# Layer a: a pair's own products moved up behind its key-value sums, ahead of the products with the state

## The chip, the cores and the metric

The kernel runs on one core of one Trainium2 chip. The metric is the time of one execution on the device, in microseconds (us). The engines are named as in the profile: PE multiplies matrices (PEld is its loading of weights), DVE, ACT and POOL are the vector, scalar and general engines, SP issues the DMAs.

## The reference

Four sub-layers with residual sums run over `x` of shape (4, 2048, 512). The change touches the first, a causal linear attention with 16 heads of 64:

```python
q = relu(x @ Wq) + EPS;  k = relu(x @ Wk) + EPS;  v = x @ Wv        # x: after layer norm
context = cumsum(einsum('bhnd,bhne->bhnde', k, v), axis=2)          # sums of keys times values
D_inv = 1.0 / einsum('bhnd,bhnd->bhn', cumsum(k, axis=2), q)
attn = einsum('bhnd,bhnde,bhn->bhne', q, context, D_inv)
x = x + attn @ Wo + bo
```

Behind it come a quantised feed-forward product, a gated linear attention with decays (layer b) and the feed-forward product again.

## The kernel before

A flag read at run time chooses between two forms of the layers; the profiled one is `layer_a_mild` and then `layer_b_mild`. Layer a ends about 2450 us into the span, layer b takes the rest.

`layer_a_mild` works on 16 blocks (`n`, 0 to 15) of 512 rows, and in each block on eight pairs of heads (`hp`, 0 to 7): 128 pairs. A block's 512 rows are four chunks of 128. The sum over earlier positions is split. What a chunk owes to earlier chunks goes through a running state per pair: `before[i]` is the state ahead of chunk `i`, and its product with the queries, four of 128x128 by 128 columns, is L968 ("the state's products" below). What a chunk owes to its own rows goes through masked scores: `scores` (L888) multiplies keys and queries, DVE multiplies the mask in (`sm`, L894, one tile for each of the two heads), and L974 multiplies the values with them ("the own products"): eight, each on 64 columns of the array, two heads side by side. Both are summed in one bank of PSUM, `pn` (one buffer, tag `n`), which ACT copies to `oT` (L983). `update` (L904) makes the sums of keys times values of each chunk, eight products on 64 columns of the array as well, which ACT copies to `u` (L909) and POOL adds up into `within` (L914, six additions), from which the state's products read.

Each f32 product stands as two PE instructions in the trace, so four of the state's products are x8 and eight of the own products x16.

`attend` returns a list of six steps for a pair: keys, scores, update, weigh, outputs, and an empty one. `spread` runs them in this order and puts one sixth of a list `fill` behind each step. `fill` holds the products that belong to no pair's chain: keys and queries of the next pair (`pk`, `pq`, four products each), values (`pv`, four), the projection of the block before (`po`, eight, for `hp` 0 to 3) or its feed-forward product (`pf`, for `hp` 4 to 7). The first `len(fill)/6` items stand behind keys, and so on. PE follows this order. On DVE, ACT, POOL and SP the order is set when the program is built, by a planner that takes what it expects to be ready first. In the trace there are steps of a later pair ahead of some of an earlier one.

For `hp` 3 and 7, `weigh` makes the divisors of four pairs: products with `same` (L926, bank `pd`), a logarithm and an exponential on ACT (L931, L933), two corrections on DVE (L935, L936), a store to DRAM (`rec`, L938) and loads that spread it over the partitions (`wide`, L959, one buffer, two pairs at a time). The four divisions `oT * wide` (L950) are put in the next pair's `fill` at places 6, 7, 13 and 15; the second one also issues the load for the last two. The projection of the block before reads the divided tiles: after `hp` 7 the four divisions lie in pair 0 of the next block, and so do the projection's first products.

Other lines that are named below: L804 takes a feature's product out of PSUM, L710 copies a tile into planes for the transposing DMA of L712, L717 joins the transposed planes (for `kr`, which `update` reads), L838 adds a projection to `x`, L124 and L125 take row statistics, L131 normalises, L664 to L670 quantise a row for the feed-forward product, L683 takes that product out, L733 loads the next block's `x`, L998 stores a finished block. In layer b, L1360 and L1373 are its update (`pub`) and outputs (`pyT`), which stand one right behind the other.

Of the kernel before, what the change touches and what calls it, by code (L numbers as in the profile page):

```python
# [10 lines left out]
F32 = mybir.dt.float32  # L11
# [8 lines left out]
P = 128  # L20
# [26 lines left out]
def hybrid_block_kernel(ctx: ExitStack, tc: tile.TileContext, t: dict, out: bass.AP):  # L47
# [4 lines left out]
    nc = tc.nc  # L52
# [16 lines left out]
    def banks(psum, **bufs):  # L69
        def bank(shape, dtype, name, tag):  # L70
            return psum.tile(shape, dtype, name=name, tag=tag, bufs=bufs[tag])

        return bank
# [97 lines left out]
    NTA = TA // P  # L171
# [464 lines left out]
    def run(steps):  # L636
        for f in steps:
            f()
# [83 lines left out]
    def layer_a_mild():  # L722
        with ExitStack() as es:
# [3 lines left out]
            bank = banks(psum, mm=3, s=2, n=1, u=1, t=1)  # L727
# [121 lines left out]
            def attend(B, hp):  # L849

                A = Block()
                chunks = [slice(i * P, (i + 1) * P) for i in range(NTA)]
                heads = [slice(h * DA, (h + 1) * DA) for h in range(2)]
                inner = within[hp % 2]
                vh = [slice((2 * hp + h) * DA % D, (2 * hp + h) * DA % D + DA) for h in range(2)]

                def v():
                    return B.v[hp // (NP // 2)]
# [97 lines left out]
                def load(rec, m):  # L956
# [2 lines left out]
                        nc.sync.dma_start(wide[r, :, :], rec[m : m + 2, h, :].partition_broadcast(DA))  # L959
                    return wide  # L960

                def outputs():


                    q = B.qk["q", hp]
                    pn = bank([P, NTA, P], F32, name="pn", tag="n")
                    for i in range(NTA):
                        nc.tensor.matmul(  # L968
                            pn[:, i, :], A.before[i], q[:, chunks[i]],
                            start=(i == 0), stop=False, skip_group_check=True,  # L970
                        )
                    for i in range(NTA):
                        for h, r in enumerate(heads):
                            nc.tensor.matmul(  # L974
                                pn[r, i, :], v()[:, i, vh[h]], A.sm[h][:, i, :],
                                start=False, stop=True, skip_group_check=True,
                            )
                    for r in heads:
                        nc.gpsimd.tensor_tensor(
                            A.before[0][r, r], A.before[NTA - 1][r, r], A.u[r, NTA - 1, :], ALU.add  # L980
                        )
                    B.oT[hp] = pool.tile([P, TA], F32, name="oT", bufs=12)
                    nc.scalar.copy(B.oT[hp], pn.rearrange("p i t -> p (i t)"))  # L983

                return [keys, scores, update, weigh, outputs, lambda: None]

            def block(n, x):
                B = Block()
                B.n, B.x, B.xn, B.qk, B.v, B.oT, B.mul, B.qc, B.kt = n, x, {}, {}, {}, {}, {}, {}, {}
                return B  # L990
# [15 lines left out]
            B, prev = block(0, x), None  # L1006
# [5 lines left out]
            for n in range(len(at)):  # L1012
# [6 lines left out]
                for hp in range(NP):  # L1019
# [20 lines left out]
                    for place, f in zip((6, 7, 13, 15), weights):  # L1040
                        fill.insert(place, f)
                    weights.clear()
                    spread(attend(B, hp), fill)
                    if n == 0:

# [10 lines left out]
                B = after if more else None  # L1056
# [640 lines left out]
```

## Time and profile before

| what | us |
|---|---|
| median of 3 runs (3968.38 to 3970.84) | 3969.62 |
| the profiled execution | 3970.43 |
| its span, first to last instruction | 3968.6 |
| PE busy in the span | 3886.1 |
| DVE busy | 2418.3 |
| POOL busy | 1504.4 |
| ACT busy | 879.2 |

The 1.8 us between the profiled execution and its span lie outside the first and last instruction. A matmul's row has a start and a modelled length; matmuls are pipelined, so what one costs is read from the start of one run of products to the start of the next.

### The profile page before, as it was taken

To read this page: it belongs to the slowest core of one execution; us is meant where nothing else is said; L and a number is where in the kernel's file an instruction comes from. 1 tells how busy PE (TensorE), PEld (TensorE's weight loads), DVE (VectorE), ACT (ScalarE), POOL (GpSimd) and SP (SyncE) were. 2 spreads that over 40 slices of the span, in tenths; PEclk is the share of its full clock that TensorE was granted. 3 is DMA by queue.
4 is the path that set the end of the run, shared out by engine and by line. 5 is a ranking of instruction groups with operands and counts; after the bars stand their busy time and mean duration, and the time that the engine had idled before them with its cause. 6 is when DMAs were issued, how large, how long until landed. Compare 5 with 4: busy or idle time off the path is not lost.

```text
span 3968.6 us, 53472 instructions
## 1 busy us (share of the span) xinstructions
PE 3886.1 (98%) x20765; PEld 2128.6 (54%) x20765; DVE 2418.3 (61%) x4552; ACT 879.2 (22%) x1550; POOL 1504.4 (38%) x2523
## 2 busy tenths in 40 slices
PE   7999999999999999999999996999999999999997
PEld 4555554555545555555555553666666666666664
DVE  4455555555555555554554554677777777777776
ACT  1221221221221221221222211222222222222221
POOL 3223323323233233233233223355555545555553
PEclk9999999999999999999999997999999999999999
DMA  4122222222212212212212214122212222222211
GB/s 139 30 41 54 67 41 54 67 40 54 67 39 55 67 39 55 67 39 55 67 39 55 57 29 144 23 54 54 55 50 51 52 53 54 55 50 51 53 37 32
DMA packets 430967, 216.97 MB, mean 55 GB/s; under 512 B 362736, under 2 KB 375920, under 8 KB 430704
## 3 DMA queue, kind: packets, MB, share of 16 engines
q1 hardware_dynamic: 429584, 211.89, 21.9%
q8 instruction: 165, 2.70, 0.3%
q10 hardware_dynamic: 1120, 1.57, 0.1%
q14 instruction: 98, 0.80, 0.1%
HBM read 91.49 MB, written 34.08 MB: 32 GB/s over the span
## 4 chain that ended last, share of the span: by engine, by line
PE 95%; DMA 2%; DVE 2%; POOL 1%; issue 0%; ACT 0%; SPq 0%; ACTq 0%; DVEq 0%; POOLq 0%
PE pr L1230 12%; PE pk L648 11%; PE pq L648 11%; PE pv L648 11%; PE po L648 11%; PE pvb L648 6%; PE py L1394 5%; PE pss L888 3%; PE ps L1326 3%; PE pn L974 3%; PE pg L648 3%; PE pl L1263 3%; PE pf L681 3%; PE pn L968 3%; PE pu L904 2%; PE pyT L1373 1%
## 5 line engine op out<-in xcount | busy, mean ns | idle before, releaser
L648 PE MATMUL pq<-xnTa,a_Wq 128*128 128x512 f32 x1024 | 492.2, 608 | 0.0
L648 PE MATMUL pk<-xnTa,a_Wk 128*128 128x512 f32 x1024 | 491.0, 604 | 0.0
L648 PE MATMUL pv<-a_Wv,xnTa 128*128 128x512 f32 x1024 | 476.6, 604 | 2.9 <-ACT xnTa L141 2.9
L648 PE MATMUL po<-a_Wo_sb,oT 128*128 128x512 f32 x1024 | 467.4, 601 | 7.2 <-DVE oT L950 7.1
L126 POOL TENSOR_SCALAR rs<-mv 128x1 f32<-128x1 f32 x320 | 82.3, 257 | 1019.4 <-DVE mv L125 1016.3
L914 POOL TENSOR_TENSOR within<-state,u 64x64 f32<-64x64 f32 x256 | 158.1, 618 | 523.4 <-ACT u L909 513.8
L648 PEld LDWEIGHTS po<-a_Wo_sb,oT 128*128 128x128 f32 x1024 | 189.3, 190 | 236.0 <-issue 220.0
L648 PEld LDWEIGHTS pv<-a_Wv,xnTa 128*128 128x128 f32 x1024 | 188.8, 191 | 234.4 <-issue 224.2
L648 PEld LDWEIGHTS pq<-xnTa,a_Wq 128*128 128x128 f32 x1024 | 181.4, 189 | 193.1 <-issue 182.8
L648 PEld LDWEIGHTS pk<-xnTa,a_Wk 128*128 128x128 f32 x1024 | 184.5, 189 | 180.9 <-issue 158.8
L909 ACT COPY u<-pu 128x256 f32<-128x256 f32 x128 | 47.7, 373 | 1026.9 <-PE pu L904 1026.9
L1230 PE MATMUL pr<-xnTb,m_kT_sb 128*128 128x256 f32 x1024 | 237.9, 385 | 0.0
L894 DVE TENSOR_TENSOR sm<-pss,causal 128x512 f32<-128x512 f32 x256 | 164.2, 683 | 119.8 <-PE pss L888 119.8
L1230 PE MATMUL pr<-xnTb,m_qT_sb 128*128 128x256 f32 x1024 | 237.2, 385 | 0.0
L717 ACT COPY kr<-turned 128x1024 uint16<-128x1024 uint16 x120 | 139.3, 1161 | 426.3 <-DMA turned<-planes 426.3
L648 PE MATMUL pvb<-b_vT_sb,xnTb 128*128 128x512 f32 x512 | 233.7, 599 | 0.0
L1394 PE MATMUL py<-b_oT_sb,yT 128*128 128x512 f32 x512 | 231.1, 594 | 0.0
L1339 DVE TENSOR_TENSOR ab<-ps,m_causal 128x512 f32<-128x512 f32 x256 | 164.1, 682 | 95.4 <-PE ps L1326 95.4
L1230 PEld LDWEIGHTS pr<-xnTb,m_qT_sb 128*128 128x128 f32 x1024 | 193.7, 192 | 32.6 <-ACT q L1294 0.2
L683 DVE SCALAR_TENSOR_TENSOR f_y<-pf,f_sc,rscale 128x512 f32<-128x512 f32 x126 | 94.5, 750 | 191.2 <-PE pf L681 191.0
L1230 PEld LDWEIGHTS pr<-xnTb,m_kT_sb 128*128 128x128 f32 x1024 | 189.4, 190 | 35.6 <-issue 12.3
L127 POOL TENSOR_TENSOR rs<-rs,neg_half 128x1 f32<-128x1 f32 x320 | 194.0, 607 | 26.3
(171 smaller groups left out, 6302.8 us busy)
## 6 DMA issues: line engine op xcount, KB each, us to landing
wide<-rec SPq DMA_DIRECT2D x124, 256.0 KB, 3.6
mmid<-xa SPq DMA_DIRECT2D x16, 1024.0 KB, 4.3
out<-xb SPq DMA_DIRECT2D x31, 512.0 KB, 2.8
xa<-in_x SPq DMA_DIRECT2D x15, 1024.0 KB, 6.6
xb<-mmid SPq DMA_DIRECT2D x30, 512.0 KB, 3.8
turned<-planes SPq DMA_TRANSPOSE x304, 3.1
m_cos<-in_cos SPq DMA_DIRECT2D x30, 128.0 KB, 2.5
m_sin<-in_sin SPq DMA_DIRECT2D x30, 128.0 KB, 2.3
```

The source lines that it names most:

```text
L127: nc.gpsimd.tensor_tensor(rs, rs, neg_half[:, :n], ALU.pow)
L648: nc.tensor.matmul(held[0], lhs(), rhs(), start=(n == 0), stop=(n == len(pairs) - 1))
L681: nc.tensor.matmul(pf, qT[:, c, :], rq[:, c, :], start=(c == 0), stop=(c == KC - 1))
L717: nc.scalar.copy(dst.bitcast(U16).rearrange("p n (t two) -> p n t two", two=2), turned.rearrange("p (two n) t -> p n t two", two=2),)
L888: nc.tensor.matmul(ps[h][:, i, :], k[r, chunks[i]], q[r, chunks[i]], start=True, stop=True)
L894: nc.vector.tensor_tensor(s, ps[h], causal.unsqueeze(1).to_broadcast([P, NTA, P]), ALU.mult)
L914: nc.gpsimd.tensor_tensor(A.before[i + 1][r, r], A.before[i][r, r], u[r, i, :], ALU.add)
L968: nc.tensor.matmul(pn[:, i, :], A.before[i], q[:, chunks[i]], start=(i == 0), stop=False, skip_group_check=True,)
L974: nc.tensor.matmul(pn[r, i, :], v()[:, i, vh[h]], A.sm[h][:, i, :], start=False, stop=True, skip_group_check=True,)
L1230: nc.tensor.matmul(pr[:, half, :], wp[name][:, c, lo : lo + P], B.xnT[:, c, :], start=(c == 0), stop=(c == KC - 1),)
L1339: nc.vector.tensor_tensor(C.a[:, half, :, :].rearrange("p h (j s) -> p h j s", s=QB), ps[half].rearrange("p j h s -> p h j s"), small["cau ...
L1394: nc.tensor.matmul(py, B.yT[i][:, c, :], wo[:, c, :], start=(c == 0), stop=(c == KC - 1))
```

## The change

The own products get a step of their own, `own`, which now opens the bank `pn` (`start` on its first products) and runs right behind `update`, with no fill between them. `outputs` keeps the state's products, which now close the bank, the last two additions to the state and the copy to `oT`. The list of steps changes too: the empty step moves up to third place, `update` with `own` is fourth, `weigh` fifth and `outputs` sixth. So update, weigh and outputs each stand one sixth of the fill later than before, and the own products one sixth earlier. No instruction is added or taken away.

```diff
+                def own():
+                    A.pn = bank([P, NTA, P], F32, name="pn", tag="n")
+                    for i in range(NTA):
+                        for h, r in enumerate(heads):
+                            nc.tensor.matmul(
+                                A.pn[r, i, :], v()[:, i, vh[h]], A.sm[h][:, i, :],
+                                start=(i == 0), stop=False, skip_group_check=True,
+                            )
+
                 def outputs():
-                    q = B.qk["q", hp]
-                    pn = bank([P, NTA, P], F32, name="pn", tag="n")
+                    q, pn = B.qk["q", hp], A.pn
                     for i in range(NTA):
                         nc.tensor.matmul(
                             pn[:, i, :], A.before[i], q[:, chunks[i]],
-                            start=(i == 0), stop=False, skip_group_check=True,
+                            start=False, stop=True, skip_group_check=True,
                         )
-                    for i in range(NTA):
-                        for h, r in enumerate(heads):
-                            nc.tensor.matmul(
-                                pn[r, i, :], v()[:, i, vh[h]], A.sm[h][:, i, :],
-                                start=False, stop=True, skip_group_check=True,
-                            )
...
-                return [keys, scores, update, weigh, outputs, lambda: None]
+                return [keys, scores, lambda: None, lambda: run([update, own]), weigh, outputs]
```

## The prediction

> **What bounds the kernel now.** I read the page's first part, the chain, and then layer a alone, by the busy time of a stretch and PE's waits.
>
> ```profile
> PE 3886.1 (98%) x20765; PEld 2128.6 (54%) x20765; DVE 2418.3 (61%) x4552; ACT 879.2 (22%) x1550; POOL 1504.4 (38%) x2523
> PE 95%; DMA 2%; DVE 2%; POOL 1%; issue 0%; ACT 0%; SPq 0%; ACTq 0%; DVEq 0%; POOLq 0%
> ```
>
> ```profile
> 166.00:2400.00 2234.00, 2230.99 (x11015) 1130.17 (x11018) 1211.89 (x2317) 484.09 (x652) 671.83 (x1428) 1.00 0.22 52
> ```
>
> ```profile
> PE po L648 <- DVE oT L950: 7.1, 4, 5.7
> PE pn L968 <- POOL within L914: 3.9, 7, 1.2
> ```
>
> In the stretch from 166 to 2400 us PE is busy 2231 of 2234 us, at a granted clock of 1.00; the next, DVE, 1212. PE's waits in all of layer a are a few us. So layer a lasts as long as PE's own sequence, and what the change does to that sequence is its effect, as long as no new wait arises. The sequence is read from the timeline of PE, here for pair 5 of a block (starts in the first column):
>
> ```profile
> 1638.93 1.88 PE L648 MATMUL pk<-xnTa,a_Wk 128*128 128x512 f32 x4
> 1640.74 1.16 PE L888 MATMUL pss<-qT,kT 64*128 64x128 f32 x16
> 1641.83 1.98 PE L648 MATMUL pk<-xnTa,a_Wk 128*128 128x512 f32 x4
> 1643.74 0.69 PE L904 MATMUL pu<-va,kr 128*64 128x64 f32 x16
> 1644.36 3.70 PE L648 MATMUL pq<-xnTa,a_Wq 128*128 128x512 f32 x8
> 1647.90 0.38 PE L968 MATMUL pn<-qT,state 128*128 128x128 f32 x2
> 1648.12 0.83 PE L968 MATMUL pn<-qT,within 128*128 128x128 f32 x6
> 1648.88 1.09 PE L974 MATMUL pn<-sm,va 128*64 128x128 f32 x16
> 1649.91 3.70 PE L648 MATMUL pv<-a_Wv,xnTa 128*128 128x512 f32 x8
> ```
>
> A 512-column instruction takes 0.43 us, a 128-column one 0.11. What is over these is the price of going between the whole array (128\*128) and parts of it (64\*128, 128\*64). Going in: 1638.93 to 1640.74 is 1.81 = 4 x 0.43 + 0.09. Coming out costs twice: own products 1.03, of which seven steps take 0.82 (1.09 less the last one's 0.27), the last pair streams 0.10, and 0.10 is idle; then the first whole-array run is 0.10 longer than its products (1641.83 to 1643.74 is 1.91 against 1.81).
>
> **What PE's sequence loses.** Before, update and own products are two excursions per pair; after, one. Per pair:
> - The idle behind update: its last product starts at 1643.74 + 0.69 - 0.23 (one product's mean) = 1644.20, the next run 0.16 later.
> - The 0.10 that the first run behind update is longer (q x8: 3.54 against 8 x 0.43 = 3.44).
> - The 0.09 of going in ahead of the own products: the state's x8 take 0.98 against 8 x 0.11 = 0.89. After the change they stand between whole-array products and cost 0.89.
> - The own products' first step is longer (0.16) than the later ones (0.10), since the second weights only load while it streams.
>
> In their place stands a join of update and own products, which layer a's trace doesn't have. Layer b has its like, also between products of 64 and of 128 columns on equal parts of the array:
>
> ```profile
> 2976.28 0.32 PE L1360 MATMUL pub<-vb,kt 128*32 128x64 f32 x8
> 2976.41 0.62 PE L1373 MATMUL pyT<-ab,vb 128*32 128x128 f32 x16
> ```
>
> The last of `pub` starts at 2976.28 + 0.32 - 0.23 = 2976.37 and `pyT` 0.04 later, and its first step is no longer than the others (0.62 - 0.27 = 0.35 for three of 0.11). So the join is bounded below by this 0.04 to 0.05 and above by a full coming out and going in, which would save nothing. I take 0.05, from the row that is the same thing in another place. The sum: 0.11 (0.16 to 0.05) + 0.10 + 0.09 + 0.05 = **0.35 us a pair**; 0.30 if the own products keep their long first step.
>
> The Trainium skill, "TensorEngine Tiling (Array Packing)", Key Properties, says that changing the tiling mode, not just the tile, drains TensorE; the rows above agree (0.09 in, 0.20 out). It would let the join through, since both sides are 128\*64.
>
> 127 pairs count (the last one's gain is hidden, below): 127 x 0.35 = 44.8 us with the unrounded 0.353.
>
> **What moves.** The empty step gives up its place, so update, weigh and outputs each run one sixth of fill later.
> - The state's products wait for POOL's six additions (`within`) seven times, in blocks 0 and 15, 3.9 us by the wait's row and 5.0 counted from start to start. From update's start to theirs there were 4.15 us in a short pair (1643.74 to 1647.90); after, the own products lie between as well, and there are 0.5 + 1.0 + 0.1 + 8 x 0.43 = 5.0. Seven waits shrink by up to 0.87 us each, in five pairs: -3.6 us.
> - The bank `pn` has one buffer and is now taken at the own products. The pair before leaves it after its state's products and one ACT copy of 0.59; between lie a sixth of fill, scores and two more, over 8 us. Nothing.
> - `kr` has one buffer and update frees it later, by 1.7 to 3.4 us. The next pair's transposed keys land some 4 us after update (ACT waits for the DMA then, 3.5 to 3.9 us), so ACT waits for the DMA as before. Nothing; without that cover u's copy would be late by what is missing.
> - The masks (L894) must be done when the own products come, now 4.2 us after the scores (four items and update) where it was 7 or more. In pairs 5 to 7 the masks end 1.5 us after the scores, in pairs 1 to 3 3.1 with 6.8 allowed, in pair 0 3.7 with 5.9. Covered, but for pair 4 (rivals).
> - weigh starts later. Behind the last pair nothing hides it: PE waits 5.7 us there for the divisions. From the scores to `pd` it was 2394.93 to 2399.60; after, 1.09 + 6 items' instructions 2.77 + 0.52 + 0.97 + 1.91 = 7.26, so **+2.6 us**, once.
>
> Sum: -44.8 - 3.6 + 2.6 = -45.8 us. From the profiled execution, 3970.4 - 45.8 = 3924.6; the runs' median lies 0.8 below that execution. **Forecast 3925 us**.
>
> **The rivals.** All but the last two lie in weigh being later, counted from `pd` (after pairs 3 and 7). Here is DVE behind pair 3, where `pd` started at 1596.38:
>
> ```profile
> 1610.31 0.69 DVE L950 TENSOR_TENSOR oT<-oT,wide 128x512 f32<-128x512 f32 x1 [6.29 <-DMA wide<-rec]
> 1610.92 0.68 DVE L838 TENSOR_TENSOR xa<-po,xa 128x512 f32<-128x512 f32 x1
> ...
> 1614.67 0.69 DVE L664 TENSOR_REDUCE f_sc<-f_xn 128x1 f32<-128x512 f32 x1
> 1615.27 1.28 DVE L894 TENSOR_TENSOR sm<-pss,causal 128x512 f32<-128x512 f32 x2
> ```
>
> The planner put the first division ahead of L838 and the masks, and DVE stood 6.3 us for its load, which lands 13.5 to 14 us after `pd`. PE didn't mind: own products came at 1618.98, masks ended at 1616.55. After the change pair 4's scores start 9.8 us after `pd` (0.99 + 2.68 + 0.89 + 3.43 + 1.81) instead of 13.6, and its own products 15.05 after `pd`.
>
> (1) *DVE keeps this order: slower.* The masks then end 5.2 to 5.8 + 3.8 = 9.0 to 9.6 us after the scores, the own products want them at 4.2, and PE waits some 5 us in 15 blocks: 3925 + 76 = 4001. It decides as soon as the planner thinks the load landed before L838 can run, 8.2 us after `pd` now. Against it: behind pair 7, DVE ran L683 9.4 us after `pd`, after 1.4 us of idleness, ahead of the division, so the planner didn't think it landed by then. Chance 0.08.
>
> (2) *The division slips in between L838 and the masks.* It needs a planned landing between 9.4 and 10.7 us. The first division at 13.5, quantising and masks end near 16.5 against 15.05: 1.5 x 15 = 22, 3947. The planner's landing lies below 12.0 (it went ahead of L838 there) and behind pair 7 of block 0 above 11.9 (kT's L804 went first), so most of it speaks for masks first. Chance 0.16.
>
> (3) *The last two divisions at a block's start.* Behind pair 7:
>
> ```profile
> 1083.24 1.14 DVE L876 SCALAR_TENSOR_TENSOR qc<-qc,ksum,qT 128x128 f32<-128x128 f32 x4
> 1088.31 1.29 DVE L124 BATCH_NORM_STATS2 st<-xa 128x6 f32<-128x512 f32 x2 [3.93 <-DMA xa<-in_x]
> ...
> 1091.21 2.35 DVE L950 TENSOR_TENSOR oT<-oT,wide 128x512 f32<-128x512 f32 x2
> ```
>
> They end 0.9 us too late to 1.3 early for the projection that reads them, which comes 3.3 us earlier after `pd` after the change (28.9 to 25.6). If their chain keeps its length, 13 boundaries cost 13 x 3.3 less the slack, 36 us net: 3961. I hold it shorter: they stand behind statistics of the next x, whose load (L733, 1081.43) stood behind L712, planes and kT's eviction, behind the first divisions. After the change the next keys are done 9.8 us after `pd`, before those divisions' load lands, and the block's store, which frees the buffer, goes some 3 us earlier. Chance 0.12.
>
> (4) *The own products' first weights aren't loaded under update.* Then the join costs their load, 0.137 us (median of the LDWEIGHTS rows of `pn<-sm,va`), and the long first step stays: 0.35 - 0.14 - 0.05 = 0.16 a pair, 3949. Against it: the join in layer b, and own steps of 0.10, shorter than one load. The Trainium skill, "TensorE: Matmul & The Clock Gate", Part 3, The mechanism, has such a rule: a weight load overlaps running matmuls only if its row group differs, and both steps use all rows; by that rule, 3949, and these rows speak against it. Chance 0.04.
>
> (5) *The join costs what the two ways cost*, so the change doesn't do what it says: 3970.4 - 3.6 + 2.6 = 3969. Chance 0.04.
>
> **How the numbers follow.** The forecast has 0.56 (3919 to 3932: the 0.05 of the first step either way, and the 2 us of po's waits that may go), then 0.16, 0.12, 0.08, 0.04, 0.04. A range of 3919 to 3962 leaves out (1) and (5), 0.12, and part of (3). A measurement can tell some 0.2%, 8 us: faster means under 3961.7. Case (3) lies on that edge and is split. Faster 0.82, same 0.10, slower 0.08.
>
> **What would show it.** `pn<-sm,va` starting about 0.05 us after the last `pu`, runs behind update gone from 3.54 to 3.44, state's x8 at 0.89; a short pair of 15.03 us instead of 15.38. In pair 4, masks ahead of the first division. It is wrong if PE waits for `sm` at the own products, or for L950 at `po`, in most blocks.

## The result, and the profile after the change

The changed kernel takes 3954.93 us (median of 8 runs, 3946.81 to 3964.18), the kernel before 3969.64 on the same chip (median of 8, 3968.38 to 3971.49): a ratio of 0.9965, with an interval of 0.9956 to 0.9973. It is faster by 14.7 us, a third of the 45 that were forecast. The runs also spread over 17 us where those of before spread over 3, which suggests that something on the kernel's path now varies from run to run. The profiled execution took 3948.51 us, its span 3946.7.

The first part of the page and the chain that ended last:

```profile
PE 3842.0 (97%) x20643; PEld 2107.2 (53%) x20765; DVE 2406.3 (61%) x4552; ACT 883.6 (22%) x1550; POOL 1453.2 (37%) x2523
PE 87%; DMA 6%; DVE 4%; POOL 1%; issue 1%; ACT 1%; SPq 0%; POOLq 0%; DVEq 0%; ACTq 0%
```

PE's busy time is 44 us down (the trace has 122 records fewer, too), but its share of the chain fell from 95% to 87%: DMA stands in the chain three times as much as before, DVE twice. The busy time of layer a's stretch (start and end, length, then PE busy, PEld, DVE, ACT, POOL, the granted clock, the DMA share and GB/s) says the same. PE idled 3 us in it before, and idles 22 now, at the same clock:

```profile
160.00:2374.90 2214.90, 2193.21 (x10955) 1110.03 (x11012) 1200.43 (x2317) 489.81 (x653) 624.34 (x1433) 1.00 0.23 53
```

PE's waits (total us, times, longest) name the place:

```profile
PE po L648 <- DVE oT L950: 23.9, 23, 7.2
PE pn L977 <- POOL within L914: 1.4, 4, 0.6
```

The wait for POOL's additions shrank from 3.9 us, as forecast. The projection's wait for the divisions (L950) went from 7.1 us in 4 places to 23.9 in 23. Of these, 5.7 and 7.2 are the one at layer a's end that the prediction counted; the rest went from 1.4 to 16.7 us.

Here is the short pair on PE (start, duration, engine, line, tiles):

```profile
1768.33 1.16 PE L888 MATMUL pss<-qT,kT 64*128 64x128 f32 x16
...
1773.05 0.69 PE L904 MATMUL pu<-va,kr 128*64 128x64 f32 x16
1773.56 1.04 PE L968 MATMUL pn<-sm,va 128*64 128x128 f32 x16
1774.54 1.98 PE L648 MATMUL pq<-xnTa,a_Wq 128*128 128x512 f32 x4
1776.36 1.88 PE L648 MATMUL pv<-a_Wv,xnTa 128*128 128x512 f32 x4
1778.08 0.38 PE L977 MATMUL pn<-qT,state 128*128 128x128 f32 x2
1778.30 0.83 PE L977 MATMUL pn<-qT,within 128*128 128x128 f32 x6
1778.97 1.88 PE L648 MATMUL pv<-a_Wv,xnTa 128*128 128x512 f32 x4
...
1783.36 1.16 PE L888 MATMUL pss<-qT,kT 64*128 64x128 f32 x16
```

The last `pu` starts at 1773.05 + 0.69 - 0.23 = 1773.51 and the own products 0.05 later. They take 1773.56 to 1774.54, 0.98 us where they took 1.03, so their first step is no longer than the others. The four products behind them take 1.82 and the next four 1.72, so one run, not two, is 0.10 longer than its products. The state's products take 1778.08 to 1778.97, 0.89. From scores to scores it is 15.03 us. In the kernel before it was 15.38, from 1640.74 (in the prediction) to the next pair's:

```profile
1656.12 1.16 PE L888 MATMUL pss<-qT,kT 64*128 64x128 f32 x16
```

Every term of the 0.35 us is there, and the pairs in which no wait changed are 0.34 to 0.35 shorter.

What is new stands at a block's start. Here is DVE (the idle time before a group and its releaser stand in brackets) behind a pair 7 whose `pd` started at 1940.22:

```profile
1955.85 1.14 DVE L876 SCALAR_TENSOR_TENSOR qc<-qc,ksum,qT 128x128 f32<-128x128 f32 x4
1964.03 1.29 DVE L124 BATCH_NORM_STATS2 st<-xa 128x6 f32<-128x512 f32 x2 [7.04 <-DMA xa<-in_x]
...
1966.93 2.35 DVE L950 TENSOR_TENSOR oT<-oT,wide 128x512 f32<-128x512 f32 x2
```

And the products that read the two divisions, on PE:

```profile
1967.67 1.12 PE L648 MATMUL po<-a_Wo_sb,oT 128*128 128x512 f32 x2 [1.67 <-DVE oT L950]
1969.34 1.12 PE L648 MATMUL po<-a_Wo_sb,oT 128*128 128x512 f32 x2 [0.55 <-DVE oT L950]
```

DVE had nothing to do for 7 us, then took the statistics of the next block's `x` and only then the last two divisions. PE needed these 2.2 us earlier. The SP queue's issues show that the divisions' own loads were not what DVE stood for: the last `wide` load was issued at 1956.77, and such a load lands 3.8 us later (median), so at about 1960.6 by estimate. Followed back, the chain of waits (start, duration) goes through the block's store and the load of the next `x`:

```profile
1950.07 6.24 DMA mmid<-xa
...
1956.33 7.68 DMA xa<-in_x
...
1964.03 1.29 DVE st L124 x2
```

`xa` has three buffers. The load (L733) goes into the one that the store frees, so it can't go before the store has landed, and the statistics wait for the load. What held the load up changed, though. Here are SP's issues at one block's start before (behind the pair 7 of the prediction's view under rival (3)), and at the one above after:

```profile
1072.67 1.25 SPq L959 DMA_DIRECT2D wide<-rec  x2
1074.57 0.40 SPq L998 DMA_DIRECT2D mmid<-xa  x1
...
1080.09 1.29 SPq L712 DMA_TRANSPOSE turned<-planes  x1
1081.43 0.58 SPq L733 DMA_DIRECT2D xa<-in_x  x1
```

```profile
1948.72 1.25 SPq L959 DMA_DIRECT2D wide<-rec  x2
1950.07 0.54 SPq L1001 DMA_DIRECT2D mmid<-xa  x1
1951.64 2.15 SPq L712 DMA_TRANSPOSE turned<-planes  x1
1955.11 0.59 SPq L959 DMA_DIRECT2D wide<-rec  x1
1956.33 0.40 SPq L733 DMA_DIRECT2D xa<-in_x  x1
1956.77 0.58 SPq L959 DMA_DIRECT2D wide<-rec  x1
```

Before, the store was issued 0.03 us after the end of POOL's addition that completes the block (L684), and the load 0.05 us behind the issue of L712, at every such start. After, the store is issued 0.10 us behind weigh's second `wide` load, 0.8 to 1.2 us after that addition, and L712 is out of the load's way. The load is released by the store's landing, 5.6 to 7.6 us after the store's issue, at all 13 starts, and the last `wide` load stands behind it on SP.

Medians over 12 of these 13 starts (without the first), counted from the end of the block's last `pf` product, in us:

| | before | after |
|---|---|---|
| `pd` starts | -9.23 | -6.29 |
| store issued | 2.33 | 3.57 |
| `x` load issued | 8.44 | 10.22 |
| statistics start | 14.73 | 17.07 |
| last division ends | 19.98 | 22.33 |
| PE's product that reads it | 20.52 | 22.38 |

Without a wait that product stands at 20.18 (its place in experiment 1 below). Before, the chain ended about when PE came; now it ends 2.2 us late. Nearly all of the loss lies there: the pair that begins a block takes 20.18 us from scores to scores without the wait, and 20.53 to 22.93 in these blocks of the profile after, 23.0 us too much over 13 blocks (2.9 before, against its own 20.52). Of the other pairs, three pairs 7 are 0.7 to 0.8 us too long, and one pair 2 by 0.3.

### The profile page after: what moved, and what is told of

The parts are those of the page before. It is cut to its first block, busy times and chain, and to the rows that moved or that the text cites. A ratio compares the mean times of both kernels' runs of the same rounds, so it can differ in the third digit from the quotient of the medians.

```text
span 3946.7 us, 53375 instructions
## 1 busy us (share of the span) xinstructions
PE 3842.0 (97%) x20643; PEld 2107.2 (53%) x20765; DVE 2406.3 (61%) x4552; ACT 883.6 (22%) x1550; POOL 1453.2 (37%) x2523
## 4 chain that ended last, share of the span: by engine, by line
PE 87%; DMA 6%; DVE 4%; POOL 1%; issue 1%; ACT 1%; SPq 0%; POOLq 0%; DVEq 0%; ACTq 0%
PE pr L1233 12%; PE pk L648 10%; PE pq L648 10%; PE po L648 9%; PE pv L648 9%; PE pvb L648 6%; PE py L1397 5%; PE ps L1329 3%; PE pss L888 3%; PE pg L648 3%; PE pl L1266 3%; PE pn L968 2%; PE pf L681 2%; DMA xa<-in_x 2%; PE pn L977 2%; DMA mmid<-xa 2%
## 5 line engine op out<-in xcount | busy, mean ns | idle before, releaser
L648 PE MATMUL po<-a_Wo_sb,oT 128*128 128x512 f32 x1024 | 472.5, 598 | 25.1 <-DVE oT L950 23.9
L648 PE MATMUL pv<-a_Wv,xnTa 128*128 128x512 f32 x1024 | 490.4, 602 | 2.9 <-ACT xnTa L141 2.9
L648 PE MATMUL pq<-xnTa,a_Wq 128*128 128x512 f32 x1024 | 479.8, 600 | 0.0
L914 POOL TENSOR_TENSOR within<-state,u 64x64 f32<-64x64 f32 x256 | 86.0, 336 | 403.1 <-ACT u L909 393.5
L914 POOL TENSOR_TENSOR within<-within,u 64x64 f32<-64x64 f32 x512 | 203.7, 398 | 36.3
L838 DVE TENSOR_TENSOR xa<-po,xa 128x512 f32<-128x512 f32 x64 | 44.2, 691 | 257.7 <-PE po L648 257.7
```

Of the source, the lines that this page charges most:

```text
L648: nc.tensor.matmul(held[0], lhs(), rhs(), start=(n == 0), stop=(n == len(pairs) - 1))
L914: nc.gpsimd.tensor_tensor(A.before[i + 1][r, r], A.before[i][r, r], u[r, i, :], ALU.add)
```

## The experiments

The theory: the joins gave all 45 us, and at each block's start the last two divisions, which DVE keeps behind the next `x`'s statistics, came late through the chain store, load, statistics. The rival: the divisions' own `wide` loads come late because weigh starts later, and DVE's order doesn't matter. A second rival: the join saves less than the pair's rows show, since something else in layer a got longer.

**1. The next `x` is loaded later.** The creation of the next block, with its load, moves from ahead of the pair loop into it, ahead of pair 1. So the planner meets the statistics after the divisions.

```diff
-                if more:
-                    after = block(n + 1, load_x(n + 1))
                 for hp in range(NP):
+                    if more and hp == 1:
+                        after = block(n + 1, load_x(n + 1))
```

> The changed kernel, but the next block's x is loaded at the start of pair 1 instead of ahead of pair 0. The theory (at a block's start the last two divisions stand on DVE behind the statistics of the next x, and these wait for its load, which waits for the store of the block two before): DVE then has the divisions ahead of the statistics, PE's waits for L950 at po fall from 23.9 us to under 3, time 3924 to 3931 us, and the runs lie within some 3 us of each other instead of 17. The rival (the divisors themselves come too late, since weigh starts later): waits for L950 stay near 20 us and the time near 3950.

Measured: 3925.16 us (3925.07 to 3926.39), ratio 0.9889 (0.9874 to 0.9904), and the spread of the runs is down to 1.3 us. PE's only wait for the divisions is the one at layer a's end, which the expected 3 us had left out, and DVE at a block's start takes the divisions first:

```profile
PE po L648 <- DVE oT L950: 7.5, 1, 7.5
```

```profile
1944.36 1.29 DVE L950 TENSOR_TENSOR oT<-oT,wide 128x512 f32<-128x512 f32 x2 [3.94 <-DMA wide<-rec]
1947.29 1.29 DVE L124 BATCH_NORM_STATS2 st<-xa 128x6 f32<-128x512 f32 x2 [1.63 <-DMA xa<-in_x]
```

The load of `x` comes no sooner than in the kernel after (statistics start at 17.49 against 17.07 in the table's terms), yet the last division ends at 15.52 instead of 22.33. Two things changed: DVE's order, and on SP the last `wide` load, which no longer stands behind the load of `x` and is issued 1.3 us sooner. The second can't be what counts: at the start shown above, that load had landed at 1960.6 by the estimate, while DVE stood idle until 1964.03, and both divisions, 2.4 us together, would have been done before PE came for them at 1966.0. So the rival that the `wide` loads come late falls.

With this wait taken away the change comes to the forecast's 3925, in part by luck. Between the profiled executions before and here, the pairs are 46.1 us shorter (48.4 were forecast) and the end 4.0 longer (2.6), but the first scores also come 3.1 us sooner, which no forecast had.

**2. Weigh in its old place.** The joined step stays, weigh stands right ahead of it.

```diff
-                return [keys, scores, lambda: None, lambda: run([update, own]), weigh, outputs]
+                return [keys, scores, lambda: None, lambda: run([weigh, update, own]), lambda: None, outputs]
```

> The changed kernel, but weigh stands ahead of update in the fourth step, about where it was before the change; update, own products and outputs stay. The rival (weigh's later start is what costs): waits for L950 at po under 3 us, 3925 to 3945 us (up to 18 us for pair 4, where the planner takes the first division ahead of the masks again). The theory (the chain runs over store, load of x and statistics, of which weigh only holds the store up by about 1 us in SP's queue): waits for L950 at po still 6 to 12 us, and 3935 to 3960 us with pair 4's waits for the masks.

Measured: 3937.54 us (3934.36 to 3941.26), ratio 0.9922 (0.9908 to 0.9935).

```profile
PE po L648 <- DVE oT L950: 6.6, 3, 5.6
PE pn L968 <- DVE sm L894: 8.1, 12, 1.2
```

In the table's terms, the store is issued at 2.39, the load at 8.09, the statistics start at 14.51 and the last division ends at 19.76: the times of before, and PE's wait is nearly gone. So it is weigh's place that delays the chain, as the rival had it: of the 6.6 us, 5.6 are the wait at layer a's end, and 1.0 is left at the blocks' starts. The theory had the store's delay about right (1.2 us, 3.57 to 2.39), but not that the load and the statistics come 2.1 and 2.6 us sooner with it. Experiments 1 and 2 go together: weigh's later place makes the chain end late, and the divisions suffer from it because DVE has them behind the statistics. The 12 us over experiment 1 are another wait: the first two divisions again stand ahead of pair 4's masks on DVE, and the own products, which now come early, wait for those. Counted from start to start these waits are 19.2 us, 1.4 in each of 14 blocks; the pairs 3 and 7 are 0.19 shorter each, 5.7 us, and the end is 2.6 shorter. 19.2 - 5.7 - 2.6 = 10.9, of 11.1 us between the two profiled executions; smaller differences of both signs are not followed up.

**3. The shift without the join.** The kernel before, with its empty step moved up, so that update, weigh and outputs (with both groups of products) each come one sixth later.

```diff
-                return [keys, scores, update, weigh, outputs, lambda: None]
+                return [keys, scores, lambda: None, update, weigh, outputs]
```

> The kernel before with only the steps moved: the empty step third, update fourth, weigh fifth, outputs with the own products behind the state's products sixth. The theory (the gain is the join alone, the loss comes with the later places): no gain in the pairs, 15.38 us for a short pair as before, waits at po 10 to 25 us, so 3975 to 3992 us. The rival (the later places gain too, by shorter waits, and the join gives less than 0.35 us a pair): 3945 to 3968 us.

Measured: 3980.77 us (3974.99 to 3986.76), ratio 1.0027 (1.0016 to 1.0038), with a wide spread again:

```profile
PE po L648 <- DVE oT L950: 13.6, 13, 7.3
```

The shift alone loses 11 us and wins nothing: a short pair takes 15.38 us as before. So what the change gains is the join. What it loses begins with the shift, but the join adds to it: it brings PE sooner to the products that read the divisions, and the wait is 23.9 us with it, 13.6 without.

**4. The joined step one place earlier.**

```diff
-                return [keys, scores, lambda: None, lambda: run([update, own]), weigh, outputs]
+                return [keys, scores, lambda: run([update, own]), weigh, outputs, lambda: None]
```

> The changed kernel with the old places of the steps: update with the own products third, weigh fourth, outputs fifth, the empty step last. The theory: a short pair still takes 15.03 us, so the join is worth its 44 us, but the own products now come 2.5 to 3.4 us after the scores and wait for the masks in pair 4 (some 2 us in 15 blocks) and pair 0 (some 1 us), and waits at po stay near 10 us: 3960 to 3985 us. If the masks do not hold it up: 3928 to 3940 us.

Measured: 4047.16 us (4044.74 to 4049.61), ratio 1.0194 (1.018 to 1.0208). The mechanism is the expected one, the size is a miss, more than twice what was expected. In pair 4 DVE runs two divisions ahead of the masks, as the prediction's rival (1) has it, and in pair 0 one of them. DVE in a pair 4, where the scores had started at 1503.26:

```profile
1507.68 1.29 DVE L950 TENSOR_TENSOR oT<-oT,wide 128x512 f32<-128x512 f32 x2 [4.61 <-DMA wide<-rec]
...
1510.60 1.28 DVE L894 TENSOR_TENSOR sm<-pss,causal 128x512 f32<-128x512 f32 x2
```

The scores were done at 1504.4, more than 3 us before the division started, and in between DVE waited for a DMA on its behalf. From start to start, PE waits 73.0 us for the masks in the pairs 4 (3.9 to 6.5 in 14 blocks, 1.1 in the last), about the 76 of rival (1), and 25.8 in the pairs 0. With experiment 1 as the measure, layer a's pairs are 124.7 us longer; masks make 99.9 of it. About 9 more are the wait for the divisions at the blocks' starts. The rest stands in the pairs 4 and goes with the granted clock. Here are PE's next products and a stretch of the busy times (start and end, length, then PE busy, PEld, DVE, ACT, POOL, the granted clock, the DMA share and GB/s) in the same pair:

```profile
1511.43 1.89 PE L968 MATMUL pn<-sm,va 128*64 128x128 f32 x16 [3.62 <-DVE sm L894]
1513.24 4.20 PE L648 MATMUL pq<-xnTa,a_Wq 128*128 128x512 f32 x6
```

```profile
1512.60:1516.00 3.40, 3.40 (x10) 1.52 (x7) 3.40 (x8) 0.00 (x0) 0.00 (x0) 0.50 0.30 58
```

Around the end of PE's wait the granted clock falls to 0.50, for 3.4 or 6.8 us, in the pairs 4 of 14 blocks, 68 us in all; in experiment 1 it is 1.00 from 160 to 2350 us. Products of 512 columns step at up to 0.86 us there instead of 0.43, and in the 14 pairs they lose 18 us by it. So a long wait of PE cost more here than its own length, which no estimate had.

**5. The kernel before with the later load.** The edit of experiment 1, alone.

> The kernel before, with the next block's x loaded at the start of pair 1. The theory: the late load only takes away waits that stand in the way of po, of which the kernel before has 2 us, so 3964 to 3970 us: the late load alone is no gain, it only lets the change's gain through. The rival (the 30 us between the changed kernel and its form with the late load are the late load's own gain, in any order of steps): near 3940 us.

Measured: 3967.04 us (3963.83 to 3968.93), ratio 0.9991 (0.9982 to 1.0). By itself the later load is worth some 3 us at most; the interval reaches 1. Without it the change gains 14.7 us; with it, about 41 (ratios 0.9991 and 0.9889, from two sets of runs on two chips; 41.5 between the profiled executions). The order that hardly cost anything before is what the change ran into.

**6 and 7. The join, by itself.** Both kernels have the later load and a list of seven steps. In 6 update and own products are one step; in 7 they are two steps with a seventh of the fill between. DVE's order is the same in both.

```diff
-                return [keys, scores, lambda: None, lambda: run([update, own]), weigh, outputs]
+                return [keys, scores, lambda: None, lambda: run([update, own]), lambda: None, weigh, outputs]
```

> The changed kernel with the late load, and a further empty step ahead of weigh (seven steps, fill in sevenths): the pair to the next run, with update and the own products joined. The theory: the join's gain doesn't hang on the exact places, 3922 to 3932 us.

```diff
-                return [keys, scores, lambda: None, lambda: run([update, own]), weigh, outputs]
+                return [keys, scores, lambda: None, update, own, weigh, outputs]
```

> As the run before, seven steps and the late load, but the own products are a step of their own, one seventh of fill behind update, with whole-array products between them. The theory: the two ways between the whole array and its halves are back, 0.35 us in each of 128 pairs, so 42 to 47 us above the joined form, 3966 to 3978 us; the row from the last pu to the next run shows 0.16 us again, and the first run behind it 0.10 more. The rival (the join is worth little, the gain comes from the places): within 15 us of the joined form.

Measured: 3936.45 us (3934.64 to 3937.71) joined, ratio 0.9913 (0.99 to 0.9927), and 3975.9 (3974.43 to 3976.73) split, ratio 1.0015 (1.0006 to 1.0024). The split costs 39.5 us over 128 pairs, 0.31 us each, under the expected 42 to 47. From scores to scores it is all there, though: 121 of 127 pairs are 0.34 to 0.35 us longer in the split kernel. The six others are so by less or not at all, and the split kernel comes to its first scores 0.9 us sooner and takes 0.6 us less behind the last. PE in the split kernel:

```profile
746.20 0.69 PE L904 MATMUL pu<-va,kr 128*64 128x64 f32 x16
746.82 1.99 PE L648 MATMUL pq<-xnTa,a_Wq 128*128 128x512 f32 x4
748.73 1.09 PE L968 MATMUL pn<-sm,va 128*64 128x128 f32 x16
```

The run behind update takes 1.91 from start to start and the own products 1.03 (748.73 to 749.76), against 1.82 and 0.98 in the kernel after. The joined kernel 6 is 11 us slower than experiment 1, which was not expected. 6.7 of it stand in the pairs 7, which take about 0.55 more than their 17.94: weigh comes later still there, and the next pair's `pk` waits for its corrections (`f_y`, L935; 4.9 us in 14 waits by the row). 2.3 stand ahead of the first scores, 1.0 behind the last; the rest is spread over other pairs.

**8. The tail.** Experiment 1, and for the last block's last pair alone weigh in its old place.

```diff
+                    if B.n + 1 == len(at) and hp == NP - 1:
+                        return [keys, scores, lambda: None, lambda: run([weigh, update, own]), lambda: None, outputs]
```

> The changed kernel with the late load, and weigh ahead of update for the very last pair alone, whose divisors nothing hides. The theory: pd of that pair comes 3.4 us earlier (3.9 us after the scores' start instead of 7.3), and the end with it: 3921 to 3923 us against 3925. If the end hangs on something else there: 3924 to 3926 us.

Measured: 3922.59 us (3921.59 to 3926.36), ratio 0.9881 (0.9866 to 0.9897). The median lies 2.6 us under that of experiment 1, the term of the prediction's tail; the intervals overlap, so that the gain is not shown by the times alone. In the profiled executions the stretch from the last scores to the end is 2.6 us shorter, and PE's wait at the end went from 7.5 to 5.8 us. This kernel has the lowest median of all, and is faster than both that were given.

## Why the prediction was wrong, point by point

- **What bounds the kernel, and the 0.35 us a pair**: right. The idleness behind update (0.16 to 0.05), one run fewer that is 0.10 too long, the state's products (0.98 to 0.89) and the own products' first step (0.05 less) came out to the hundredth, in the short pairs 15.38 to 15.03. Experiments 6 and 7 give 0.34 to 0.35 in 121 of 127 pairs, 0.31 by whole runs.
- **That the join costs 0.05**, taken from layer b: right (0.05). So rivals (4) and (5) are out. The rule behind rival (4), in the Trainium skill, "TensorE: Matmul & The Clock Gate", Part 3, The mechanism (a weight load overlaps running matmuls only if its row group differs), does not hold for these rows: update and own products use all rows, the load takes 0.137 us, and the step from one to the other 0.05. The same section also has loads into the background weight buffer pulled ahead, and the rows agree with that: the own products' first weights load at 1773.51, where the last `pu` starts.
- **POOL's additions**: 3.9 to 1.4 us by the row; the pairs that had these waits are 2.9 us shorter, of the 3.6 forecast.
- **The masks, and rivals (1) and (2)**: neither came. PE waits for `sm` nowhere in the kernel after, and in pair 4 DVE runs the masks first:

```profile
2034.81 0.69 DVE L838 TENSOR_TENSOR xa<-po,xa 128x512 f32<-128x512 f32 x1
...
2039.09 1.27 DVE L894 TENSOR_TENSOR sm<-pss,causal 128x512 f32<-128x512 f32 x2
2041.02 1.29 DVE L950 TENSOR_TENSOR oT<-oT,wide 128x512 f32<-128x512 f32 x2 [0.66 <-DMA wide<-rec]
```

  How little was missing, experiments 2 and 4 show: with the divisions ahead of the masks 1.4 and 5.1 us are lost in the pair 4 of a block, on the average of 14 blocks.
- **The last two divisions at a block's start, rival (3)**: this step failed. The prediction had the place, the rows and the deadline (3.3 us earlier after `pd`), and a price of 36 us, but held the case at 0.12, because "the block's store, which frees the buffer, goes some 3 us earlier" and the load had stood behind L712. L712 did go out of the load's way. But in the mean of the 13 starts, counted from `pd`, the store goes 1.4 us earlier (11.55 to 10.15), not 3, the load 1.3, and the statistics, on which the divisions wait, 1.1. The store doesn't move with `pd`. It followed POOL's addition (L684) behind the block's last `pf` product; after, weigh's two corrections run ahead of what feeds that addition on DVE (L683), which delays it by 0.4 to 1.5 us, and weigh's two `wide` loads stand ahead of the store on SP, for another 0.8 or more. And with L712 gone, the load waits for the store's landing, which comes no sooner after the store's issue than L712 had let the load go: 6.3 us in the mean, 6.2 before. The case's mechanism is what happened. Its price of 36 us was for a chain that keeps its length; with the 1.15 us by which the chain shortens, 13 starts give 21, and the blocks' starts lost 20.1 (23.0 against 2.9) in the profiled execution. That was one of the faster executions; by the medians of experiment 1 and of this kernel the whole loss is some 30 us.
- **The tail**, +2.6: from the last scores to `pd` there are 7.27 us where there were 4.68, as forecast, and experiment 8 takes as much away again.

The sum, for the profiled execution (3970.43 to 3948.51, -21.9), from scores to scores: the join in 127 pairs -43.6, POOL's additions -2.9, the divisions at the blocks' starts +20.1, the four pairs named above +2.5, together -23.9. Behind the last scores +5.4: 2.6 of the tail, 2.5 in layer b, which the change doesn't touch, and 0.3. Ahead of the first scores -3.3. This and layer b's 2.5 were in no forecast, and why they came is open.

Left open: why the times from the store to the load and from the load to the statistics vary (5.6 to 7.6 and 5.5 to 7.7 us within the one trace after), and whether it is by this that the runs of this kernel spread over 17 us, since only one execution of it has a trace. That a fourth buffer for `xa`, which would free the load from the store, takes the wait away as well wasn't tried; it takes 8 KB more of each partition.

## What to carry to other kernels

When a step is moved, write down for each instruction behind it what it stands behind on its engine, and follow that back to a DMA's landing and the buffer it waits for: here a division whose data had come stood behind statistics whose data had not. A chain that just fits is seen by its slack (-0.9 to 1.3 us here) before the change, and a kernel whose runs begin to spread may have such a chain on its path. When PE's work shrinks by as much as was forecast and the time doesn't, look for the place where the waits grew, and first reorder what waits there: the edit that was worth 3 us at most before the change was worth 30 after it. And where an edit moves the queues of other engines, read those too: here the store's place behind weigh's loads on SP is part of what the forecast had missed.

## What the runs showed of the hardware

A second change between products of 128 and of 64 columns costs PE 0.35 us in f32 here: 0.09 going in, 0.11 more idleness coming out (0.16, against the 0.05 of two joined groups), a first run behind it that is 0.10 longer, and 0.05 in the first step. Two groups of 64 columns that differ in the number of elements streamed join in 0.05.

The granted clock fell to 0.50 for 3.4 or 6.8 us around the end of PE's waits of 3.9 to 6.5 us in 14 blocks of experiment 4; at its waits for masks of up to 2.2 us in the pairs 0 it stayed at 1.00.

That the runs of a kernel that is 97% PE can spread by 17 us (0.4%) with one DMA chain on its path, and by 1.3 us in the four runs with the chain off it, was not expected. The runs of experiment 2, with 1 us of these waits left, still spread by 7, so the chain may not be all of it.
